# Router logits tied behind counted shared products, 2.5 units of shared work moved ahead of the last chunk's routing

## The chip, the cores and the metric

The kernel runs on one core of a Trainium2 chip. The metric is device time in microseconds (us), the median of three timed executions. Besides these there is one execution under the hardware profiler, from which all views of the profile come. Engines are called PE (TensorE matrix products; PEld its weight loads), DVE (VectorE), ACT (ScalarE), POOL (GpSimd) and SP (SyncE).

## The reference

Input `x` is 16 x 256 rows of 256 numbers, 4096 rows in all. First a spiking layer changes `x`, then a mixture of experts with one shared expert is added to it. All is float32.

```python
rates = relu(x) * 0.001
c  = cond[:, None, :] + cumsum(rates, axis=1)      # along the 256 steps
fl = floor(c);  x = x + (fl - previous fl) / 0.001 # previous of step 0: floor(cond)

shared = silu(x @ w1) * (x @ w3) @ w2              # 256 -> 512 -> 256
s      = sigmoid(concat([x, cond]) @ router_W)     # 8 experts
top2   = top_k(s + router_bias, 2)
gates  = s[top2] / sum(s[top2])                    # 1/2 each if the sum is about 0
y_e    = gelu(x @ W1e[e]) @ W2e[e]                 # 256 -> 256 -> 256
out    = x + (shared + sum over top2 of gates * y_e) / 3
```

## The kernel before

The rows go in eight chunks of 512 (`NCHUNK`). Three kinds of work are interleaved on the engines.

`elementwise(i)` makes the spikes of a chunk: PE turns `x` (L294), ACT makes rates, DVE scans them, floors, differences and adds. The last step (L389, two halves) writes `x1`, with the features on the partitions.

`route(i)` is the routing of a chunk, as a generator that is advanced step by step: logits `pl` on PE (L535, 16 records), on DVE their bound `lt` (L544), a transpose `pn` on PE (L547), Exp on ACT (L551), the choice of two experts on DVE (L553 to L590, ending with `hot`), counts `pr` on PE (L596 to L602), transposes `px` of the rows on PE with copies to `x1t` on ACT (L618, L619), the places `at_i` on DVE (L624 to L632), and at last eight indirect DMAs on POOL (L636), which scatter rows with their tags to the buffer `xs` in device memory, grouped by expert. The tag column is copied by POOL out of `key_first` (L571, L573). `key_first`, `at_i` and `lt` lie in the pool `rt` with two buffers each.

The shared expert is one generator, `all_shared`: hidden products of chunk i (L659: four pairs of products a chunk, each pair followed by Silu on ACT, L669, and a product on DVE, L670), then output products of chunk i-1 (L686, with an addition on DVE, L697). `unit(n)` advances it by n units: a unit is one pair of hidden products of 512 columns (four calls of matmul, eight records of the profile, since a float32 product is two), or one half of a chunk's output (eight calls, sixteen records). There are 48 units, or 288 calls. Units are the filling with which PE is kept at work while other engines prepare something.

What sets the order: in the loop `for i in range(2, NCHUNK)` the framework's scheduler orders each engine's instructions. It takes them by their place in the program and by when it thinks their inputs are ready, so a product that stands later in the program may be put ahead. The start and the last part stand under `manual_schedule`, where PE, DVE and ACT keep the written order. Each engine then runs its list strictly in order: an instruction that waits holds all behind it.

The last part begins with the routing of chunk 7: its logits, 0.5 unit, the score transpose and the choice, 2 units, counts, then `pcnt` (L866), the number of rows of each expert. From it DVE makes a table of blocks of 128 rows of one expert (L873 to L917), PE spreads it (`pcode` L920, `prow` L924), and SP writes eight pieces of zeros behind the experts' rows (L883). Between the table and `pcode` stand 2.5 units, behind `prow` 3 units, and one more in `run_blocks`. Then come 67 blocks: loads `xb` of a block from `xs` in four DMAs on SP and ACT (L956), which have to wait for the scatters' landing and the table; on DVE a copy of weights (L971) and a transpose `xbt` (L976); products `phe` (L1003); Gelu on ACT (L1011); products `py` (L1025); an indirect DMA of the result on POOL (L1034). A tail does the remaining units and adds everything up.

Of the kernel before, what the change touches and what calls it, by code (L numbers as in the profile page):

```python
# [13 lines left out]
F32 = mybir.dt.float32  # L14
BF16 = mybir.dt.bfloat16
I32 = mybir.dt.int32
# [15 lines left out]
P = 128  # L32
N = 512
SEG = 16
TOPK = 2
# [3 lines left out]
def kernel(  # L39
# [34 lines left out]
    J = N // P  # L74
    G = KD * NB
    NCHUNK = NT // N
    NTT = NT // P
    NSEG = T // SEG
    NBLK = NT * TOPK // P + E - 1
# [438 lines left out]


    placed = {}  # L520

    def route(i):
        x1, x1t = x1s[i], x1ts[i]

        def small(tag, shape=(P, J, E), dt=F32):
            return rt.tile(list(shape), dt, tag=tag, name=f"{tag}_{i}")

        def wide(a):
            return a[:, :, None].to_broadcast([P, J, E])


        pl = p_t.tile([P, P], F32, tag="pt", name=f"pl_{i}")
        for k in range(KD):
            for j in range(J):
                nc.tensor.matmul(  # L535
                    pl[ts(j, 32), :],
                    lhsT=rw[:, k, :],
                    rhs=x1[:, k, ts(j, P)],
                    start=(k == 0),
                    stop=(k == KD - 1),  # L540
                )
        yield
        lt = small("lt", (P, P))
        nc.vector.tensor_scalar(lt, pl, rc[:, i : i + 1], LOWEST, ALU.add, ALU.max)  # L544
        yield
        pn = p_t.tile([P, J, 32], F32, tag="pt", name=f"pn_{i}")
        nc.tensor.transpose(pn.rearrange("p j e -> p (j e)"), lt, ident)  # L547

        s = sig[:, ts(i, J), :]
        ex = small("ex")  # L550
        nc.scalar.activation(ex, pn[:, :, :E], AF.Exp, scale=-1.0)  # L551
        yield
        nc.vector.tensor_scalar(ex, ex, 1.0, None, ALU.add)  # L553
        nc.vector.reciprocal(s, ex)
        sel = small("sel")
        nc.vector.tensor_tensor(sel, s, rb[:, None, :].to_broadcast([P, J, E]), ALU.add)

        def best_places(sc, q):

            best = small(f"best{q}", (P, J))  # L560
            nc.vector.tensor_reduce(best, sc, AX.X, ALU.max)
            key = small(f"key{q}")
            nc.vector.tensor_tensor(key, sc, wide(best), ALU.is_equal)
            return key


        hots = [chosen[:, q, ts(i, J), :] for q in range(TOPK)]
        key = best_places(sel, 0)
        nc.vector.tensor_tensor(key, key, order, ALU.mult)
        key_first = small("first", (P, J))  # L570
        nc.vector.tensor_reduce(key_first, key, AX.X, ALU.max)  # L571
        nc.vector.tensor_tensor(hots[0], key, wide(key_first), ALU.is_equal)
        nc.gpsimd.tensor_copy(  # L573
            x1t[:, :, :, FQ + 1], key_first[:, :, None].to_broadcast([P, J, NQ])
        )
        sel2 = small("sel2")
        nc.vector.scalar_tensor_tensor(sel2, hots[0], -BIG, sel, ALU.mult, ALU.add)
        key = best_places(sel2, 1)
        run = small("run")
        nc.vector.tensor_tensor_scan(  # L580
            run.rearrange("p j e -> p (j e)"),
            keep_e,
            key.rearrange("p j e -> p (j e)"),
            0.0,
            ALU.mult,
            ALU.add,
        )
        nc.vector.scalar_tensor_tensor(hots[1], run, 1.0, key, ALU.is_equal, ALU.mult)
        hot = small("hot", dt=BF16)
        nc.vector.tensor_tensor(hot, hots[0], hots[1], ALU.add)  # L590
        yield

        pr = p_t.tile([P, J, E], F32, tag="pt", name=f"pr_{i}")
        nc.tensor.matmul(pr, lhsT=ones_r, rhs=region[0:1], start=True, stop=False)  # L596
        nc.tensor.matmul(pr, lhsT=before_b, rhs=hot, start=False, stop=False)
        for d in range(1, J):
            nc.tensor.matmul(
                pr[:, d:, :], lhsT=ones_b, rhs=hot[:, : J - d, :], start=False, stop=False  # L600
            )
        nc.tensor.matmul(  # L602
            pr,
            lhsT=ones_b,
            rhs=counts_b[i % 2][:, None, :].to_broadcast([P, J, E]),
            start=False,
            stop=True,
        )
# [13 lines left out]
        yield  # L622
        mine = small("mine", (P, TOPK, J, E))
        nc.vector.tensor_tensor(  # L624
            mine,
            chosen[:, :, ts(i, J), :],
            pr[:, None].to_broadcast([P, TOPK, J, E]),
            ALU.mult,
        )
        at_i = small("at_i", (P, TOPK, J), I32)  # L630
        with nc.allow_low_precision(reason="one whole number and zeros are added"):
            placed[i] = nc.vector.tensor_reduce(at_i, mine, AX.X, ALU.add)  # L632
        yield
        for j in range(J):
            for q in range(TOPK):
                nc.gpsimd.indirect_dma_start(  # L636
                    out=xs_w[(i * J + j) * TOPK + q][:, :],
                    out_offset=bass.IndirectOffsetOnAxis(ap=at_i[:, q, j : j + 1], axis=0),
                    in_=x1t[:, j].rearrange("p g f -> p (g f)"),
                    in_offset=None,  # L640
                )
        yield
# [5 lines left out]
    def shared_hidden(i, slices):  # L648

        ht = hts[i] = hid.tile([P, KS, N], F32, tag="ht", name=f"hs_{i}")  # L650
        x1 = x1s[i]
        for cols in slices:
            n = cols.stop - cols.start
            for u in range(KS):
                ps = []
                for w in (w1_sb, w3_sb):
                    ph = p_h.tile([P, n], F32, tag="ph", name=f"ph_{i}_{u}_{cols.start}_{len(ps)}")
                    for k in range(KD):
                        nc.tensor.matmul(  # L659
                            ph,  # L660
                            lhsT=w[:, k, ts(u, P)],
                            rhs=x1[:, k, cols],
                            start=(k == 0),
                            stop=(k == KD - 1),
                        )
# [11 lines left out]
    def shared_out(i):  # L677
# [4 lines left out]
        for h in range(J // n):  # L682
            pa = p_acc.tile([P, n, D], F32, tag="acc", name=f"pa_{i}_{h}")
            for q in range(n):
                for s in range(KS):
                    nc.tensor.matmul(  # L686
                        pa[:, q, :],
                        lhsT=ht[:, s, ts(n * h + q, P)],
                        rhs=w2_sb[:, s, :],
                        start=(s == 0),  # L690
                        stop=(s == KS - 1),
                    )
                yield 0.5, q == n - 1
# [135 lines left out]
    for i in range(2, NCHUNK):  # L829
# [12 lines left out]
        next(el, None)  # L842
        next(ro)
        next(nxt, None)
        unit(1 + (i > 3 and i % 3 != 2) + (i == NCHUNK - 1))
        next(ro)
        next(el, None)
        next(ro)
# [60 lines left out]
    table = const.tile([P, 2], I32)  # L909
    nc.vector.tensor_copy(table, table_f)  # L910

    diag = const.tile([P, P], BF16)
    nc.vector.tensor_scalar(which, which, -1.0, float(E), ALU.mult, ALU.add)
    nc.vector.tensor_scalar(diag, ident, which, None, ALU.mult)

    rows_f = const.tile([P, NBLK], F32)
    nc.vector.tensor_scalar(rows_f, ident[:, :NBLK], table_f[:, 0:1], None, ALU.mult)  # L917
    unit(2.5)
    pcode = p_t.tile([P, NBLK], F32, tag="pt", name="pcode")
    nc.tensor.matmul(pcode, lhsT=ones_b, rhs=diag[:, :NBLK], start=True, stop=True)  # L920
    code = const.tile([P, NBLK], F32)
# [2 lines left out]
    nc.tensor.matmul(prow, lhsT=ones_f, rhs=rows_f, start=True, stop=True)  # L924
    rows_i = const.tile([Q, NBLK + 1], I32)
    nc.vector.tensor_copy(rows_i[:, :NBLK], prow)
    unit(3)


    block, groups, first_rows = {}, {}, {}  # L930
# [269 lines left out]
```

## Time and profile before

| what | value |
|---|---|
| median of three timed runs | 332.89 us (332.87 to 333.72) |
| the profiled execution's own time | 342.67 us |
| its span, first to last instruction | 341.0 us |
| PE busy | 326.5 us, 96% |
| DVE busy | 225.3 us, 66% |
| ACT, POOL busy | 142.1 us, 162.8 us |
| chain that ended last: PE, DVE, ACT | 68%, 16%, 5% |
| first logits of chunks 2 to 7 on PE, at | 51.0, 69.5, 88.1, 102.8, 117.9, 136.5 us |
| first block product at | 170.3 us |
| hidden and output products of the tail, from | 292.8 us |

Times in the profile are counted from the first instruction. The profiled execution is some 10 us longer than the timed ones, so a wait that it shows need not be in these. A busy engine is one with an instruction running; for PE the matmuls' ends are modelled. In brackets behind an instruction stands how long its engine was idle before it, and what released it. "issue" means a wait for nothing that the profile shows.

### The profile page before, as it was taken

Reading aid. Unit: us, or ns where it says so; the run is one execution under the profiler, and the core shown is the slowest. Engines: PE = TensorE matmul, PEld = TensorE weight load, DVE = VectorE, ACT = ScalarE, POOL = GpSimd, SP = SyncE. Lnnn points to the kernel's source line nnn. Section 1 sums busy time; section 2 is a strip of 40 time slices with the busy share of each in tenths; the row PEclk is TensorE's granted clock in tenths of the full one; section 3 lists DMA queues with packets and bytes.
Section 4 is the critical chain, followed back from the end, with each engine's and each line's share of the span. In section 5 each row is a group of like instructions: output and inputs, shape, how many; then the busy total and the mean of one; then the engine's idle time right before and its main releaser. Section 6 shows DMA issues by size and latency. Waiting matters only on the chain.

```text
span 341.0 us, 6640 instructions
## 1 busy us (share of the span) xinstructions
PE 326.5 (96%) x1734; PEld 238.1 (70%) x1734; DVE 225.3 (66%) x612; ACT 142.1 (42%) x301; POOL 162.8 (48%) x199
## 2 busy tenths in 40 slices
PE   8899999789999999999999999999999989999996
PEld 3878544435654754855789999999999879566485
DVE  5787889677999896552277755554554543079993
ACT  4449394709487563041044444444443434310200
POOL 6000762766668887344035555555555445323220
PEclk9999999959999999999999999999999999999999
DMA  7570847643221222134446666675666553399933
GB/s 228 161 180 8 233 111 171 189 141 106 100 80 63 95 81 79 64 111 157 75 89 149 156 143 156 152 165 120 158 141 156 127 138 86 92 377 405 407 132 123
DMA packets 62550, 50.36 MB, mean 148 GB/s; under 512 B 42622, under 2 KB 52879, under 8 KB 62512
## 3 DMA queue, kind: packets, MB, share of 16 engines
q1 hardware_dynamic: 42928, 26.21, 30.0%
q0 software_dynamic: 7456, 20.86, 16.8%
q10 hardware_dynamic: 12128, 2.86, 4.8%
q8 instruction: 15, 0.25, 0.3%
q14 instruction: 23, 0.19, 0.2%
HBM read 27.44 MB, written 22.84 MB: 147 GB/s over the span
## 4 chain that ended last, share of the span: by engine, by line
PE 68%; DVE 16%; ACT 5%; issue 4%; DMA 2%; SPq 2%; another core or an unknown queue 1%; ACTq 0%; DVEq 0%
PE ph L659 21%; PE py L1025 15%; PE phe L1003 14%; PE pa L686 13%; DMA xb<-xs 2%; DVE tb L323 2%; SPq L956 2%; ACT tb L347 2%; DVE x L381 2%; DVE x L389 1%; DVE hs L670 1%; DVE tb L337 1%; PE pl L535 1%; ACT L551 1%; PE px L618 1%
## 5 line engine op out<-in xcount | busy, mean ns | idle before, releaser
L659 PE MATMUL ph<-x,w_sb 128*128 128x512 f32 (+2 forms) x320 | 121.2, 520 | 1.7 <-DVE x L487 0.8
L1034 POOL DMA_INDIRECT ys<-yb,to x67 | 66.4, 991 | 69.4 <-ACT yb L1033 51.9
L636 POOL DMA_INDIRECT xs<-x1t,at_i x64 | 76.5, 1195 | 46.4 <-issue 18.3
L659 PEld LDWEIGHTS ph<-x,w_sb 128*128 128x128 f32 x320 | 54.3, 193 | 45.0 <-issue 39.2
L1003 PEld LDWEIGHTS phe<-xbt,w1e 128*128 128x128 f32 x536 | 70.3, 191 | 4.7 <-ACT hbt L1011 0.9
L1003 PE MATMUL phe<-xbt,w1e 128*128 128x128 f32 x536 | 70.7, 275 | 0.7 <-DVE xbt L976 0.7
L1025 PE MATMUL py<-we,hbt 128*128 x268 | 69.1, 381 | 2.3 <-ACT hbt L1011 2.3
L686 PE MATMUL pa<-w_sb,hs 128*128 128x256 f32 x256 | 59.7, 383 | 0.0
L971 DVE COPY w1e<-we 128x512 f32 x67 | 29.1, 434 | 44.4 <-issue 29.9
L686 PEld LDWEIGHTS pa<-w_sb,hs 128*128 128x128 f32 x256 | 47.4, 190 | 9.5 <-issue 3.8
L669 ACT ACTIVATE as<-ph 128x512 f32<-128x512 f32 (+2 forms) x40 | 20.5, 515 | 73.8 <-PE ph L659 66.9
L1025 PEld LDWEIGHTS py<-we,hbt 128*128 128x128 f32 x268 | 45.8, 191 | 6.3 <-ACT hbt L1011 2.7
L1011 ACT ACTIVATE hbt<-phe 128x256 f32<-128x256 f32 x67 | 25.8, 385 | 47.5 <-ACT yb L1033 21.2
L670 DVE TENSOR_TENSOR hs<-as,ph 128x512 f32<-128x512 f32 (+2 forms) x40 | 23.0, 574 | 29.8 <-PE ph L659 20.7
L1033 ACT COPY yb<-py 128x256 f32<-128x256 f32 x67 | 25.0, 372 | 23.3 <-issue 17.4
L976 DVE STREAM_TRANSPOSE xbt<-xb 128x256 f32<-128x256 f32 x67 | 29.3, 437 | 1.3 <-DMA xb<-xs 0.7
L323 DVE TENSOR_TENSOR_SCAN tb<-keep,rates 128x1024 f32<-128x1024 f32 (+1 forms) x9 | 17.3, 1925 | 0.0
L712 POOL DMA_DIRECT2D out_dram<-yc x8 | 5.8, 727 | 22.7 <-DVE yc L1141 22.7
L573 POOL COPY x1t<-first 128x16 f32<-128x16 f32 x8 | 4.2, 526 | 25.0 <-DVE first L571 25.0
L347 ACT ACTIVATE tb<-tb,cond_t 128x256 f32<-128x256 f32 x30 | 13.1, 498 | 6.4 <-DVE tb L337 6.4
L697 DVE SCALAR_TENSOR_TENSOR x1t<-pa,x1t 128x512 f32<-128x512 f32 x14 | 9.6, 684 | 8.2 <-PE pa L686 8.2
L619 ACT COPY x1t<-px 128x512 f32<-128x512 f32 x16 | 8.9, 586 | 7.3 <-PE px L618 7.3
(152 smaller groups left out, 279.5 us busy)
## 6 DMA issues: line engine op xcount, KB each, us to landing
xb<-xs SPq DMA_DIRECT2D x184, 33.0 KB
yc<-ys SPq DMA_DIRECT2D x8, 512.0 KB
we<-ys SPq DMA_DIRECT2D x8, 512.0 KB
xn<-in_x_dram SPq DMA_DIRECT2D x7, 512.0 KB
xb<-xs ACTq DMA_DIRECT2D x84, 33.0 KB
we<-in_L_cond_W1e_dram SPq DMA_DIRECT2D x8, 256.0 KB
we<-in_L_cond_W2e_dram SPq DMA_DIRECT2D x8, 256.0 KB
out_dram<-yc POOLq DMA_DIRECT2D x8, 256.0 KB
```

The source lines that it names most:

```text
L323: nc.vector.tensor_tensor_scan(cs, keep[:, : cs.shape[1]], self.cut(self.rates, part), 0.0, ALU.mult, ALU.add)
L636: nc.gpsimd.indirect_dma_start(out=xs_w[(i * J + j) * TOPK + q][:, :], out_offset=bass.IndirectOffsetOnAxis(ap=at_i[:, q, j : j + 1], axis=0),
L659: nc.tensor.matmul(ph, lhsT=w[:, k, ts(u, P)], rhs=x1[:, k, cols], start=(k == 0), stop=(k == KD - 1),)
L670: nc.vector.tensor_tensor(ht[:, u, cols], act, ps[1], ALU.mult)
L686: nc.tensor.matmul(pa[:, q, :], lhsT=ht[:, s, ts(n * h + q, P)], rhs=w2_sb[:, s, :], start=(s == 0), stop=(s == KS - 1),)
L971: nc.vector.tensor_copy(w, we[:, bass.ds(off, KD * HE)])
L976: nc.vector.transpose(xt.rearrange("p g k r -> p g (k r)"), block[b].pop("xb")[:, :, :FQ])
L1003: nc.tensor.matmul(ph[:, m, :].rearrange("p (g r) -> p g r", r=Q), lhsT=w[:, k, ts(m, P)], rhs=xt[:, :, k, :], start=(k == 0), stop=(k == ...
L1011: nc.scalar.activation(ht, ph, AF.Gelu)
L1025: nc.tensor.matmul(py, lhsT=ht[:, k, :], rhs=we[:, bass.ds(off + KD * HE + k * D, D)], start=(k == 0), stop=(k == KH - 1),)
L1033: nc.scalar.copy(yb, py)
L1034: nc.gpsimd.indirect_dma_start(out=ys_w[b][:, :], out_offset=bass.IndirectOffsetOnAxis(ap=to[:, b : b + 1], axis=0), in_=yb, in_offset=Non ...
```

## The change

Four things are done.

1. Every shared product is counted as it is written down (`made`). The logits of chunks 2 to 6 get an order-only dependency on a counted product: chunk 2 comes behind the 84th, chunk 3 behind the 100th, then the 120th, 140th and 156th. No semaphore and no instruction is added; it binds the scheduler's order on PE.
2. In the loop, iterations with `i > 2` take half a unit more: 2.5 units over five iterations. The last part takes 2.5 less: 1.5 in place of 2.5 ahead of `pcode`, 1.5 in place of 3 behind `prow`. All of the loop's units stand ahead of the last chunk's logits on PE.
3. `key_first` and `at_i` get eight buffers in place of two.
4. `diag` and `rows_f` take buffers of the tag `lt` in place of their own.

```diff
+    logits = {i: [] for i in range(NCHUNK)}
+    STEP = {2: 84, 3: 100, 4: 120, 5: 140, 6: 156}
+    made = []
+
+    def in_step(i):
+        if i in STEP and logits[i] and len(made) >= STEP[i]:
+            for m in logits[i]:
+                tc.add_manual_dep(
+                    m.ins,
+                    made[STEP[i] - 1].ins.name,
+                    mybir.DependencyInfo(
+                        mybir.DependencyClass.NoSync, mybir.DependencyReason.DATA
+                    ),
+                    reason="order on TensorE",
+                )
+
+    def shared_matmul(*args, **kwargs):
+        made.append(nc.tensor.matmul(*args, **kwargs))
+        for i, n in STEP.items():
+            if n == len(made):
+                in_step(i)
...
-                nc.tensor.matmul(
+                logits[i].append(nc.tensor.matmul(
...
+        in_step(i)
         yield
...
-        key_first = small("first", (P, J))
+        key_first = small("first", (P, J), bufs=NCHUNK)
...
-        at_i = small("at_i", (P, TOPK, J), I32)
+        at_i = small("at_i", (P, TOPK, J), I32, bufs=NCHUNK)
...
-                        nc.tensor.matmul(
+                        shared_matmul(
                             ph,
...
-                    nc.tensor.matmul(
+                    shared_matmul(
                         pa[:, q, :],
...
-        unit(1 + (i > 3 and i % 3 != 2) + (i == NCHUNK - 1))
+        unit(1 + (i > 2) / 2 + (i > 3 and i % 3 != 2) + (i == NCHUNK - 1))
...
-    diag = const.tile([P, P], BF16)
+    diag = rt.tile([P, P], BF16, tag="lt", name="diag")
...
-    rows_f = const.tile([P, NBLK], F32)
+    rows_f = rt.tile([P, NBLK], F32, tag="lt", name="rows_f")
...
-    unit(2.5)
+    unit(1.5)
     pcode = p_t.tile([P, NBLK], F32, tag="pt", name="pcode")
...
-    unit(3)
+    unit(1.5)
```

More of the change, by code (lines that the diff above doesn't have):

```diff
@@ L520, with small @@
     placed = {}
+    logits = {i: [] for i in range(NCHUNK)}
[17 more added lines that the diff above has]
+                in_step(i)
     def route(i):
         x1, x1t = x1s[i], x1ts[i]
-        def small(tag, shape=(P, J, E), dt=F32):
-            return rt.tile(list(shape), dt, tag=tag, name=f"{tag}_{i}")
+        def small(tag, shape=(P, J, E), dt=F32, **kw):
+            return rt.tile(list(shape), dt, tag=tag, name=f"{tag}_{i}", **kw)
         def wide(a):
@@ L534, in route @@
             for j in range(J):
[L535 to L540, printed above, removed]
+                logits[i].append(
+                    nc.tensor.matmul(
+                        pl[ts(j, 32), :],
+                        lhsT=rw[:, k, :],
+                        rhs=x1[:, k, ts(j, P)],
+                        start=(k == 0),
+                        stop=(k == KD - 1),
+                    )
                 )
+        in_step(i)
         yield
```

## The prediction

> **What bounds the kernel now.** I read the page's head first, then TensorE's busy time stretch by stretch, then the timeline of each engine round the edited places, and last the row of one line. All fences are of the profiled execution of the kernel before.
>
> The head of the page, and two stretches of the table by windows (columns: stretch, its length, then busy time of PE, PEld, DVE, ACT, POOL with counts, granted clock, DMA share, GB/s):
>
> ```profile
> span 341.0 us, 6640 instructions
> PE 326.5 (96%) x1734; PEld 238.1 (70%) x1734; DVE 225.3 (66%) x612; ACT 142.1 (42%) x301; POOL 162.8 (48%) x199
> ...
> 60.00:70.00 10.00, 6.91 (x33) 3.63 (x30) 6.52 (x20) 5.74 (x10) 5.92 (x7) 0.95 0.76 206
> 70.00:80.00 10.00, 10.00 (x37) 4.68 (x36) 6.36 (x11) 3.49 (x7) 8.13 (x6) 0.70 0.31 110
> ```
>
> TensorE is the bound: 14.5 us idle in 341. The clock column gives what else it lost: 0.95 and 0.70 over two stretches of 10 us mean 1 + 6 = 7 us at half speed, so 3.5 us. The change adds and removes no product, so it can only move these 18 us.
>
> **The profiled execution is not the timed one.** It took 342.67 us, of which 1.7 lie outside the span; the median is 332.89, so a timed span is near 331.2, which is 9.8 us less. Matmuls at full clock can't get shorter, so those 9.8 us are idle and slow-clock time that timed runs don't have. Of the 18 us, the start (2.2 us in the first 10 us, 0.2 after) and the tail (3.2 us) make 5.6 that the program's shape forces. That leaves 18.0 - 9.8 - 5.6 = **2.6 us of TensorE idle** in a timed run between 20 and 338 us: nothing in the middle can gain more. One stall shows what was lost in the profile alone; the timeline of PE round the edits follows (start, length, line, what, count, [idle before <- releaser]):
>
> ```profile
> 65.62 1.02 PE L659 MATMUL ph<-x,w_sb 128*128 128x512 f32 x2
> 69.50 0.64 PE L535 MATMUL pl<-x,rw 128*32 128x128 f32 x4 [2.86 <-DVE at_i L632]
> ...
> 117.88 0.41 PE L535 MATMUL pl<-x,rw 128*32 128x128 f32 x4 [0.81 <-DVE x L389]
> ...
> 136.46 0.65 PE L535 MATMUL pl<-x,rw 128*32 128x128 f32 x16
> ...
> 145.97 0.40 PE L596 MATMUL pr<-region,ones_r 1*128 1x32 f32 x2
> ...
> 147.38 8.83 PE L659 MATMUL ph<-x,w_sb 128*128 128x512 f32 x20
> 156.04 0.20 PE L920 MATMUL pcode<-diag,ones_b 128*128 128x71 bf16 x1
> ...
> 156.41 3.70 PE L659 MATMUL ph<-x,w_sb 128*128 128x512 f32 x8
> 159.95 7.07 PE L686 MATMUL pa<-w_sb,hs 128*128 128x256 f32 x32
> 166.85 3.60 PE L659 MATMUL ph<-x,w_sb 128*128 128x512 f32 x8
> 170.29 1.05 PE L1003 MATMUL phe<-xbt,w1e 128*128 128x128 f32 x8
> 172.08 1.13 PE L1003 MATMUL phe<-xbt,w1e 128*128 128x128 f32 x8 [0.74 <-DVE xbt L976]
> ```
>
> The logits of chunk 3 stood 2.86 us in the middle of a hidden product, and the slow clock followed: 2.86 + 3.5 = 6.4 us. It cannot be in the timed runs: 5.6 + 6.4 alone would need 12 of the 18 - 9.8 = 8.2 us there are.
>
> The other engines at the hand-over from routing to the expert blocks, from their timelines, and the SP row of the loads' line (shortest/median/longest ns, first and last start):
>
> ```profile
> 131.58 1.29 DVE L389 SCALAR_TENSOR_TENSOR x<-x,xt 128x512 f32<-128x512 f32 x2
> ...
> 148.47 0.97 POOL L636 DMA_INDIRECT xs<-x1t,at_i  x1 [6.54 <-DVE ends L890]
> ...
> 157.40 0.97 POOL L636 DMA_INDIRECT xs<-x1t,at_i  x1 [0.30 <-issue]
> ...
> L956 SPq DMA_DIRECT2D xb<-xs x184: 3/316/1857, 160.0 to 282.3; - x184
> ```
>
> Spikes of the last chunk are ready at 132.87, but its logits run at 136.46, behind a backlog of shared products. From there a chain runs: logits, choice, places (147.0), eight scatters on POOL (148.47 to 158.37), their landing, block loads from 160.0, transpose, first block product. Shared products cover it on TensorE.
>
> **The parts, and their cost.**
>
> *Unit price.* 20 hidden records take 8.66 us (147.38 to 156.04), 0.433 each; 32 of L686 take 6.9, 0.216 each. A unit is 8 of the first or 16 of the second: 3.46 us. 2.5 units are **8.65 us**. Each hidden unit also carries one Silu on ACT (0.52) and one product on DVE (0.57 to 0.69), each output unit a DVE addition (0.68); no DMA goes with them here. ACT and DVE, 42% and 66% busy, hide these; uncovered, the 2.5 units' DVE part would be about 1.7 us.
>
> *Ties.* An order on one engine issues nothing. Counting calls (two records each) down the PE rows, logits of chunks 2 to 6 ran after 76, 90, 107, 122 and 140 shared products; they must now come after 84, 100, 120, 140 and 156, which is 5.2, 6.9, 9.1, 10.4 and 12.1 us more of shared work ahead (0.865 a hidden call, 0.432 an output call). Behind them on TensorE come the score transpose, the counts and the px transposes; for these wait Exp on ACT, the choice on DVE, and eight scatters on POOL (8 x 1.27 = 10.2 us a chunk). Late next: chunk 6's places move from 128.4 to about 140, so its scatters end near 150; the last chunk's start near 157. That cover is 7 us. Gain: the 0.81 before chunk 6's logits surely goes. The waits for `hot` before the counts (0.55, 0.23, 0.39) and one of 0.17 before a score transpose need not. Bounds: 0 to 2.15 us gained; a new static order could equally lose 1. I take **-0.8**.
>
> *A tile per chunk.* The rows of L571 and L632 show 0.7 and 0.2 us of idle in all over eight chunks each, and no DMA as releaser: nothing to gain, **0**. diag and rows_f take over `lt` buffers, last read by the score transpose at 138.86; diag is written at 150.48, rows_f at 150.68, with 11 us to spare: 0.
>
> *2.5 units moved.* The logits of the last chunk are written out behind all loop units: they move from after 160 calls to after 178, the cover of the chain shrinks by the same work (1 unit before pcode, 1.5 behind it), and the total is unchanged. Cover before: 136.46 to 170.29 = 33.8 us. After: 33.8 - 8.65 = **25.2**. Need: SP issues block 0's three loads from 160.02 to 161.92, and a load lands about 1.6 us after its issue (first update of the 160.02 load at 161.59); 0.5 for the transpose gives 164.0, so 164.0 - 136.46 = **27.6 us**. This need does not shrink: choice (hot ends 143.2) is still hidden by the two units ahead of pr, though Exp comes some 1.2 us later behind a Silu, and POOL's ten us are serial. So TensorE waits 27.6 - 25.2 = **+2.4 us** at the first block. Slack before was 6.3; that is what hid it. The wait of 0.74 at block 1 stays: DVE does block 0's transpose, then a shared product, then block 1's copy in the written order. Moved past: the scatters on POOL, eight zero stores and 184 loads on SP, 84 loads on ACT all start 8.65 us later against TensorE's work.
>
> *What is late next.* After the hand-over no slack is left. SP's 184 issues span 122.3 us, 0.668 each; 11 serve four blocks, so 1.84 us a block, against 1.76 for TensorE (174.07 to 175.83 between block products). Over 66 blocks SP loses 5.3 us of the old 6.3, harmlessly. SP's own waits for landings are 4.4 us of it; without them it keeps 1.77. So this costs 0 (SP keeps up when not profiled) to 5.3. I take **+1.2**, near the low end, since longest issues of 1.9 us against a median of 0.3 look like single delays and not its pace.
>
> *Clock.* [...] a gap of 2.86 us was followed by 7 us at half speed. [...] by the row it would cost another 3.5. I take 0[...] and keep 3.5 for the range.
>
> **Sum:** -0.8 + 2.4 + 1.2 = **+2.8**: on the profile's own terms 341.0 to 343.8 if its other stalls came again, and on the timed median 332.9 + 2.8 = **335.7 us**.
>
> **Rivals.**
> 1. *Clock or loads make it worse* (slower): the wait at block 0 reaches 2.9 us, the clock halves as at 69 us: +2.8 + 3.5 = +6.3, 339.2; with all of SP's 5.3 in place of 1.2, 343. For it: the row at 69 us. [...]
> 2. *The cover still suffices* (no change): chain and cover differ by 2.4 in 27.6. If untraced POOL and SP issues run 10% quicker, wait and drain vanish and -0.8 stays: about 332.1 to 333.5. Against: the 0.97 us of a scatter is DMA-issuing work that repeats to 10 ns.
> 3. *Faster*: timed runs do stand at the logits of chunks 3 to 6, and the 9.8 us come from elsewhere, such as the start. Place: TensorE before L535; price up to 6.4. It decides once more than 3.6 us of it is in timed runs (2.4 + 1.2); all of it gives 332.9 + 3.6 - 6.4 = 330.1. Against: the count of 2.6 us above.
>
> **Numbers.** A timed change under 0.3% (1.0 us; the runs spread over 0.85) can't be told from none. Forecast 0.50 (own range 334 to 338), rival 1 0.21, rival 2 0.17, rival 3 0.12. Faster 0.12, same 0.17, slower 0.71. The range leaves out most of rival 3 and the end of rival 1: 331.5 to 340.5.
>
> **What would show it.** Right: last logits near 144 to 145; first load on SP near 168; idle of 2 to 3 us before the first phe, released by the transpose or by xb loads; later block products waiting on hbt or xbt behind loads; no L535 idle over 0.3. Wrong: no idle at the first phe (need overstated), or idle before the last logits released by x L389 (then the extra units fill a hole I count as none), or new idle inside the loop behind scores or counts.

## The result, and the profile after

The changed kernel takes **344.87 us** (median of four runs, 344.52 to 346.02), the kernel before 332.99 beside it: a ratio of **1.0357**, 95% interval 1.0338 to 1.0375, so 11.9 us slower. 335.7 was forecast, with a range to 340.5. The direction was right, and the place in part: the hand-over to the expert blocks, but neither the wait that grew most nor the chunk loop. The size was off by a factor of four. Three of the later runs (marked "disturbed" below) fell on executions in which the kernel before itself took 335 to 343 us and a stall of some 3 us stood in the chunk loop.

Head of the page after, and two stretches of the table by windows (stretch, length, busy PE, PEld, DVE, ACT, POOL, granted clock, DMA share, GB/s):

```profile
span 342.8 us, 6638 instructions
...
PE 325.5 (95%) x1734; PEld 238.9 (70%) x1734; DVE 225.1 (66%) x612; ACT 143.0 (42%) x301; POOL 156.8 (46%) x199
...
160.00:170.00 10.00, 7.67 (x30) 4.79 (x29) 1.85 (x4) 0.00 (x0) 2.37 (x3) 0.97 0.44 108
170.00:180.00 10.00, 5.90 (x22) 5.25 (x23) 4.31 (x14) 3.17 (x6) 1.00 (x1) 0.52 0.42 70
```

The work is the same, 1734 products. What is new lies between 166 and 180 us: TensorE idles for over 6 us and then has a granted clock of 0.52. The changed kernel's lines stand 24 to 26 further down than before (logits L535 → L559, score transpose L547 → L573, block product L1003 → L1029), except that all shared products, L659 and L686, are now recorded at the helper's line L540. TensorE's timeline:

```profile
69.99 0.18 PE L623 MATMUL pr<-hot,before_b 128*128 128x32 bf16 x1 [0.79 <-DVE hot L616]
...
87.49 0.18 PE L623 MATMUL pr<-hot,before_b 128*128 128x32 bf16 x1 [1.07 <-DVE hot L616]
...
139.68 0.64 PE L559 MATMUL pl<-x,rw 128*32 128x128 f32 x16
143.44 0.30 PE L573 MATMUL pn<-ident,lt 128*128 128x128 f32 x1 [1.20 <-DVE lt L570]
...
162.85 3.60 PE L540 MATMUL ph<-x,w_sb 128*128 128x512 f32 x8
168.36 1.23 PE L1029 MATMUL phe<-xbt,w1e 128*128 128x128 f32 x8 [1.92 <-DVE xbt L1002]
174.00 2.05 PE L1029 MATMUL phe<-xbt,w1e 128*128 128x128 f32 x8 [4.41 <-DVE xbt L1002]
```

Four groups of waits: for `hot` in the chunk loop, 1.20 us at the last chunk's score transpose, 1.92 at the first block product (2.4 were forecast), and **4.41 at the second**, where 0.74 had stood. The product behind it runs at half speed: 2.05 us for what took 1.13 in the kernel before.

The second wait is read from the other engines' timelines round the hand-over (POOL's first and last scatter of chunk 7, then ACT, then DVE):

```profile
153.05 0.98 POOL L662 DMA_INDIRECT xs<-x1t,at_i  x1 [6.31 <-DVE ends L916]
...
162.00 0.97 POOL L662 DMA_INDIRECT xs<-x1t,at_i  x1 [0.30 <-issue]
...
164.46 7.29 ACTq L982 DMA_DIRECT2D xb<-xs  x7
171.85 0.60 ACT L695 ACTIVATE as<-ph 128x512 f32<-128x512 f32 x1 [17.30 <-DMA xb<-xs]
...
167.86 0.45 DVE L1002 STREAM_TRANSPOSE xbt<-xb 128x256 f32<-128x256 f32 x1 [3.23 <-DMA xb<-xs]
172.48 0.69 DVE L696 TENSOR_TENSOR hs<-as,ph 128x512 f32<-128x512 f32 x1 [4.17 <-ACT as L695]
173.08 0.42 DVE L997 COPY w1e<-we 128x512 f32 x1
173.42 0.44 DVE L1002 STREAM_TRANSPOSE xbt<-xb 128x256 f32<-128x256 f32 x1
```

From the bottom up: block 1's transpose at 173.42 stands behind the copy and the shared expert's product `hs` in VectorE's list; `hs` waits for the Silu `as`; the Silu could have run near 164.8 (it needs the first half of the `ph` products, some 1.9 us from their start, as the next fence shows), but it stands in ScalarE's list behind **seven block loads**, the early ones of `run_blocks`. These wait for the scatters: the first starts at 164.46, 1.49 us behind the end of the last one on POOL (162.97), and the seven take 7.29 us to issue. So seven DMA issues hold up one Silu by 7.1 us, and through VectorE's order a block product that does not use it. That is **theory Q** of the expectations. **Theory C** is its companion: the clock that the idle brings down costs a few us more (2.0 us, measured below).

The same place in the kernel before, from a second profile of it unchanged (span 331.7, clock 1.0; two lines each of ACT, DVE and PE):

```profile
153.10 5.71 ACTq L956 DMA_DIRECT2D xb<-xs  x7
161.86 0.60 ACT L669 ACTIVATE as<-ph 128x512 f32<-128x512 f32 x1 [9.74 <-DMA xb<-xs]
...
163.65 0.69 DVE L670 TENSOR_TENSOR hs<-as,ph 128x512 f32<-128x512 f32 x1 [1.62 <-PE ph L659]
...
164.58 0.44 DVE L976 STREAM_TRANSPOSE xbt<-xb 128x256 f32<-128x256 f32 x1
...
159.94 3.60 PE L659 MATMUL ph<-x,w_sb 128*128 128x512 f32 x8
...
165.17 1.13 PE L1003 MATMUL phe<-xbt,w1e 128*128 128x128 f32 x8 [0.74 <-DVE xbt L976]
```

There ScalarE was through with its seven early loads at 158.81, 3.05 us ahead of the Silu. **That slack of 3.05 us on ScalarE is what the change used up**; the 6.3 us of slack in the prediction were those of SP and the first transpose. The loads now start 11.36 us later (153.10 to 164.46) and the shared products ahead of the Silu only 2.91 (159.94 to 162.85), so against TensorE's list the loads have moved by 8.45 us, about the price of the units. The seven issues also take 1.58 us longer (7.29 against 5.71). That makes 8.45 + 1.58 - 3.05 = 7.0 us late, where the trace has 7.1.

**The ledger**, by the idle in the trace after against that second profile of before. TensorE's idle from 20 to 300 us went from 3.16 to 12.37 us: +2.5 in the chunk loop (5.24 - 1.55 up to 150 us, less the 1.20 that comes next), +1.20 at the last score transpose, +1.92 at the first block product, +3.67 at the second (4.41 - 0.74). That is 9.3; the half clock adds some 2 (measured below). 11.3 in all, where the spans differ by 11.1 and the medians by 11.9.

### The profile page after: what moved, and what is told of

It is laid out like the page before. It is cut to its first block, busy times and chain, and to the rows that moved or that the text cites. A ratio compares the mean times of both kernels' runs of the same rounds, so it can differ in the third digit from the quotient of the medians.

```text
span 342.8 us, 6638 instructions
## 1 busy us (share of the span) xinstructions
PE 325.5 (95%) x1734; PEld 238.9 (70%) x1734; DVE 225.1 (66%) x612; ACT 143.0 (42%) x301; POOL 156.8 (46%) x199
## 3 DMA queue, kind: packets, MB, share of 16 engines
q10 hardware_dynamic: 12128, 2.86, 4.8%
## 5 line engine op out<-in xcount | busy, mean ns | idle before, releaser
L540 PE MATMUL ph<-x,w_sb 128*128 128x512 f32 (+2 forms) x320 | 118.5, 513 | 1.1 <-ACTq L1124 0.7
L662 POOL DMA_INDIRECT xs<-x1t,at_i x64 | 69.7, 1089 | 58.2 <-issue 15.9
L540 PEld LDWEIGHTS ph<-x,w_sb 128*128 128x128 f32 x320 | 53.9, 190 | 45.2 <-issue 38.8
L1029 PEld LDWEIGHTS phe<-xbt,w1e 128*128 128x128 f32 x536 | 71.9, 196 | 10.9 <-issue 4.6
L1029 PE MATMUL phe<-xbt,w1e 128*128 128x128 f32 x536 | 72.5, 279 | 6.3 <-DVE xbt L1002 6.3
L1051 PE MATMUL py<-we,hbt 128*128 x268 | 69.8, 384 | 0.1
L540 PE MATMUL pa<-w_sb,hs 128*128 128x256 f32 x256 | 59.3, 381 | 0.0
L540 PEld LDWEIGHTS pa<-w_sb,hs 128*128 128x128 f32 x256 | 47.5, 190 | 8.9 <-issue 3.2
L599 POOL COPY x1t<-first 128x16 f32<-128x16 f32 x8 | 5.4, 674 | 23.4 <-DVE first L597 23.3
```

Source lines behind the costliest of these rows:

```text
L540: made.append(nc.tensor.matmul(*args, **kwargs))
L662: nc.gpsimd.indirect_dma_start(out=xs_w[(i * J + j) * TOPK + q][:, :], out_offset=bass.IndirectOffsetOnAxis(ap=at_i[:, q, j : j + 1], axis=0),
L1029: nc.tensor.matmul(ph[:, m, :].rearrange("p (g r) -> p g r", r=Q), lhsT=w[:, k, ts(m, P)], rhs=xt[:, :, k, :], start=(k == 0), stop=(k == ...
L1051: nc.tensor.matmul(py, lhsT=ht[:, k, :], rhs=we[:, bass.ds(off + KD * HE + k * D, D)], start=(k == 0), stop=(k == KH - 1),)
```

## The experiments

Where an expectation speaks of theory Q or C, these are the two above. The runs go from the parts of the change to the hand-over, not in order of time. Ratios are against the kernel before, run beside each.

### The kernel before again

No edit; it asks what the profiled execution had that timed runs don't.

> The kernel before, unchanged, for a profile that is closer to its timed runs. All theories: 332.9 us. If the profiled execution is near 333 too, the wait of 2.86 us at the logits of chunk 3 and the 7 us of half clock behind it should be missing, and the idle of PE between 20 and 300 us should add up to 2 to 4 us. If the wait is there again in an execution of 333 us, my count of what timed runs can hold was wrong.

Measured: 333.1 against 333.07, ratio 1.0003 (0.9994 to 1.0012), span 331.7. The stall of 2.86 us ahead of chunk 3's logits and the slow clock behind it are gone, and idle between 20 and 300 us is 3.16, where the prediction had worked out 2.6. Products at full clock take as long in both profiles (8.83 us for the twenty hidden records ahead of `pcode`). So that stall belonged to one execution, and rival 3 had nothing to win.

### Tiles alone

```diff
-    STEP = {2: 84, 3: 100, 4: 120, 5: 140, 6: 156}
+    STEP = {}
-        unit(1 + (i > 2) / 2 + (i > 3 and i % 3 != 2) + (i == NCHUNK - 1))
+        unit(1 + (i > 3 and i % 3 != 2) + (i == NCHUNK - 1))
-    unit(1.5)
+    unit(2.5)
-    unit(1.5)
+    unit(3)
```

(Against the changed kernel, as all diffs here.)

> Eight buffers for key_first and at_i and the moved diag and rows_f alone; no ties, units as before. All theories: nothing, 332.6 to 333.3. If the order made for this kernel differs by chance it can be off by a us.

Measured: 332.6, ratio 0.9984 (0.9977 to 0.9991). The tiles give 0.5 us at most.

### Ties and tiles, units where they were

The same edit without the line of `STEP`.

> The changed kernel with its 2.5 units put back behind the last chunk's routing; ties and tiles stay. Theory A (the hand-over costs it: 2.5 units less cover for the last chunk's chain): the first two block products wait as before, no half clock at 170 us, 333 to 336, where the part over 333 is what the ties cost in the loop (waits of the counts on hot). Theory R (the ties cost it, by a worse order in the loop): 340 or more.

Measured: 334.8, ratio 1.0045 (1.0026 to 1.0063): the ties **cost 2.2 us** (334.8 - 332.6). The granted clock averages 1.00 over the run, and the second block product waits its old 0.74. TensorE's timeline has the loss in the chunk loop, whose idle up to 150 us is 3.50 where the tiles alone have 1.24:

```profile
69.98 0.18 PE L623 MATMUL pr<-hot,before_b 128*128 128x32 bf16 x1 [0.78 <-DVE hot L616]
...
87.38 0.18 PE L623 MATMUL pr<-hot,before_b 128*128 128x32 bf16 x1 [0.97 <-DVE hot L616]
...
110.75 0.30 PE L573 MATMUL pn<-ident,lt 128*128 128x128 f32 x1 [0.86 <-DVE lt L570]
```

The logits don't wait, but in the kernel before, profiled again, they didn't either: the 0.81 us that the prediction let the ties win was not there. What follows the logits waits more. For chunk 2's counts (69.98) the cover is thinner: 16 records of shared products stand between its last logits and them, against 22 in the kernel before, by TensorE's timelines. For chunk 3's (87.38) it is not: 30 records against 18. There the choice itself takes longer on VectorE: 7.7 us from its first step (`ex`, 79.61) to the end of `hot` (87.33), where the kernel before took 6.1 (72.70 to 78.76). Two instructions of `elementwise` for a later chunk stand between its steps:

```profile
82.48 2.29 DVE L323 TENSOR_TENSOR_SCAN tb<-keep,rates 128x1024 f32<-128x1024 f32 x1 [0.26 <-ACT rates L301]
...
85.13 1.16 DVE L337 TENSOR_TENSOR tb<-tb,tot 128x960 f32<-128x960 f32 x1
```

In the kernel before, two others stand there, of 1.20 and 1.23 us. So later logits meet other work on VectorE; that this costs the time is read off the timeline, and no run moved these instructions.

### The same ties, at the places where the logits stood

```diff
-    STEP = {2: 84, 3: 100, 4: 120, 5: 140, 6: 156}
+    STEP = {2: 76, 3: 91, 4: 108, 5: 122, 6: 141}
```

with the units put back as above. It asks whether an order written out by hand costs by itself.

> Tiles, units as before, and ties at the places where the logits stood without them, rounded up to whole hidden products: 76, 91, 108, 122, 141 in place of 84, 100, 120, 140, 156. If the ties cost through the shift of the logits (8 to 18 products later), PE's idle before the counts in the loop returns to 1.2 to 1.6 us and the time to 332.4 to 333.2. If a tie costs as such, by a worse order, 334 or more as with the ties of the change.

Disturbed: 339.09 against 337.46, ratio 1.0086 (1.0045 to 1.0127), with a wait of 3.03 us at a shared product that no other run has. Nothing follows from it for the time. Again:

> Tiles per chunk and the ties, at the places where the logits stood before (behind 76, 91, 108, 122 and 141 shared products), and no unit moved. If the loss from the ties lies in how late they put the logits: about 332.6 to 333, that is the time of the tiles alone. If an order written out by hand costs by itself: near 334.8, as with the ties at 84 to 156.

Measured: 332.19 against 333.04, ratio 0.9974 (0.9963 to 0.9984), no worse than the tiles alone. Chunk 2's counts (64.48) wait 0.17, and chunk 3's, at 81.04, not at all:

```profile
64.48 0.18 PE L623 MATMUL pr<-hot,before_b 128*128 128x32 bf16 x1 [0.17 <-DVE hot L616]
...
81.04 0.18 PE L623 MATMUL pr<-hot,before_b 128*128 128x32 bf16 x1
```

So a tie is free; **putting the logits 8 to 18 shared products later** is what costs 2.2 us.

### Units and tiles, no ties

```diff
-    STEP = {2: 84, 3: 100, 4: 120, 5: 140, 6: 156}
+    STEP = {}
```

> The changed kernel without ties: the 2.5 units are moved and the tiles are there, the scheduler orders the logits as it likes. Theory A: PE idles about 2 us before the first block product and 4 to 5 before the second, half clock for some 10 us, 341 to 345. Theory R: 336 or less.

Measured: 342.25, ratio 1.0266 (1.0234 to 1.0298): the units **cost 9.65 us** (342.25 - 332.6). Parts add up: 332.6 + 2.2 + 9.65 = 344.4, against 344.87. The hand-over is that of the changed kernel, 2.5 us earlier; ScalarE's timeline:

```profile
161.92 6.99 ACTq L982 DMA_DIRECT2D xb<-xs  x7
169.01 0.60 ACT L695 ACTIVATE as<-ph 128x512 f32<-128x512 f32 x1 [16.97 <-DMA xb<-xs]
```

The first block product waits 2.11, the second 3.96, and the granted clock averages 0.985 over the run's 340.6 us, by estimate some 10 us at half speed. All of the large loss is in the units.

### One and a half units in place of two and a half

```diff
-        unit(1 + (i > 2) / 2 + (i > 3 and i % 3 != 2) + (i == NCHUNK - 1))
+        unit(1 + (i > 4) / 2 + (i > 3 and i % 3 != 2) + (i == NCHUNK - 1))
-    unit(1.5)
+    unit(2)
-    unit(1.5)
+    unit(2)
```

with `STEP = {}`. Moving 1.5 units takes 5.2 us of cover, less than the 6.3 of slack that the prediction had found.

> Tiles, no ties, and 1.5 units moved in place of 2.5 (half a unit in each of the last three iterations; 0.5 less ahead of pcode, 1 less behind). Shift of the chain against the cover: 5.2 us. Theory Q: PE's slack at the first block is 6.3, so no wait there; ACT's last early load would end about 5.2 later than 158.8 while the unit's products end at 161.4, so the Silu comes some 2.5 us late, and block 1's product about 1 to 2.5 us: 333.5 to 335, and no half clock. A theory of a cost in proportion to the units (9.6 us for 2.5): 338.4.

Measured: 339.55, ratio 1.0204 (1.0184 to 1.0224), a miss of the expected time by over 4 us. What was right: the first block product does not wait. But the second waits 2.71, the first down product 0.94 (for Gelu, behind the same loads on ScalarE), the last score transpose 1.13, and the granted clock averages 0.990 over the run's 337.7 us, by estimate some 6.8 us at half speed. So 5.2 us of moved cover, which costs nothing by SP's slack, cost 7 (1.13 of it at the score transpose, the rest behind ScalarE's loads and by the clock), since ScalarE had only 3.05. It is the shorter slack that counts.

### A unit written one turn later: in the kernel before, and in the changed one

If the Silu and `hs` are in the way of block 1's transpose, writing the unit behind that transpose must win the 0.74 us which even the kernel before loses. With ties and units put back as above (tiles alone):

```diff
-            if b == 0:
+            if b == 1:
                 unit(1)
```

> Tiles alone (no ties, units as before), and the unit inside the block loop is written behind the second block's transpose in place of ahead of its weight copy. PE's order stays; on DVE the unit's product then stands behind block 1's copy and transpose. If the 0.74 us wait before the second block product comes from DVE's order, it goes: 331.9 against 332.6 for the tiles alone, which would be 0.3% under the kernel before. If not: 332.6.

Measured: **331.79, ratio 0.9965 (0.9952 to 0.9977)**, as expected, and faster than both kernels. VectorE, then TensorE:

```profile
161.93 0.44 DVE L1002 STREAM_TRANSPOSE xbt<-xb 128x256 f32<-128x256 f32 x1
163.28 0.69 DVE L696 TENSOR_TENSOR hs<-as,ph 128x512 f32<-128x512 f32 x1 [0.91 <-PE ph L540]
...
163.01 1.95 PE L1029 MATMUL phe<-xbt,w1e 128*128 128x128 f32 x16
```

The second transpose goes ahead of `hs`, and both blocks' products run in one piece.

The same one line in the changed kernel:

> The changed kernel, with the unit in the block loop written one turn later, so that its Silu and its VectorE product stand behind the second block's transpose. Theory Q (the wait of 4.41 us at the second block product is the Silu behind seven loads on ScalarE, handed on by VectorE's order): the second transpose no longer waits for the Silu, so the second block product waits 0 to 0.8 us. ScalarE still issues its seven loads, then the Silu, then the first Gelu, so the first down product waits for that Gelu instead, 1.5 to 2.5 us. The wait of about 2 us at the first block product stays. In all 1.5 to 3 us less than the changed kernel: 342 to 343.5. Rival (the second product waits for its block's rows or for SP's loads): its wait stays at 4 to 4.5 us, released by xbt, and the time stays at 344.5 to 345.5.

Measured: 344.4, ratio 1.0335 (1.0317 to 1.0352), no better than the changed kernel; the expectation missed, and the rival too. TensorE, ACT, DVE:

```profile
175.22 2.08 PE L1029 MATMUL phe<-xbt,w1e 128*128 128x128 f32 x8 [5.61 <-ACT as L695]
...
164.50 9.96 ACTq L982 DMA_DIRECT2D xb<-xs  x9
174.57 0.60 ACT L695 ACTIVATE as<-ph 128x512 f32<-128x512 f32 x1 [19.96 <-DMA xb<-xs]
...
169.65 0.45 DVE L1002 STREAM_TRANSPOSE xbt<-xb 128x256 f32<-128x256 f32 x1 [0.76 <-DMA xb<-xs]
```

The second transpose is done at 170.1, 5 us before the product that uses it. But a turn later there are **nine** loads ahead of the Silu, it comes 2.7 us later, and the block product now waits for the Silu itself (`as`, which has to read `ph` before its accumulator is free for another product; that this is the reason is inferred from the releaser and from the pool `p_h`, whose three buffers the shared pair and block 0 fill). The loads and rows are in time; the Silu behind loads is what binds. In the kernel before the same edit wins because ScalarE had slack.

### Fewer loads ahead of the Silu

```diff
-    AHEAD = 6
+    AHEAD = 3
```

> The changed kernel, but only three blocks' loads stand ahead of the block loop in place of six, so four loads and not seven stand before the Silu on ACT. SP's order of loads stays. Theory Q (the 4.4 us wait before the second block product is ACT's list: Silu behind seven loads, DVE's product behind Silu, block 1's copy and transpose behind that): the Silu starts near 167 in place of 171.9, the wait at block 1 falls to about 1, PE keeps its full clock, 338 to 340. Theory L (block 1's data land late): wait and clock stay, 344 to 346.

Measured: 351.25, ratio 1.0521 (1.0487 to 1.0555), far above what was expected. At the hand-over it does what theory Q says: four loads, the Silu 4.6 us earlier, and no wait at the second block product (ACT):

```profile
164.50 2.60 ACTq L982 DMA_DIRECT2D xb<-xs  x4
167.21 0.60 ACT L695 ACTIVATE as<-ph 128x512 f32<-128x512 f32 x1 [12.62 <-DMA xb<-xs]
```

But a lead of three blocks holds for the whole stage, and is too short: the groups of lines have 11.6 us of wait at block products, 9.2 of it at eight of them later than 190 us, behind transposes that wait for rows (columns: busy us, mean ns, idle before).

```profile
L1029 PE MATMUL phe<-xbt,w1e 128*128 128x128 f32 x536 | 73.2, 281 | 11.6 <-DVE xbt L1002 11.5
...
L1002 DVE STREAM_TRANSPOSE xbt<-xb 128x256 f32<-128x256 f32 x67 | 29.6, 442 | 33.5 <-DMA xb<-xs 32.7 <-SPq L1124 0.3
```

The edit did two things at once, so the next one keeps the lead of the rest of the stage.

### Loads spread over the first turns

```diff
-        for b in range(first, min(first + AHEAD, end)):
+        ready = min(first + 3, end)
+        for b in range(first, ready):
             load_block(b, first, end)
...
-            if b + AHEAD < end:
-                load_block(b + AHEAD, first, end)
+            for _ in range(2):
+                if ready < end and ready <= b + AHEAD:
+                    load_block(ready, first, end)
+                    ready += 1
```

> The changed kernel with three blocks' loads ahead of the block loop and then two blocks' loads per turn of the loop, until six blocks are ahead again. It keeps what e5_ahead3 showed at the hand-over (Silu at 167, no wait at the second block product) and not its short lead. Theory Q with the clock as seen: the wait at the first block product stays at about 2, that at the second is under 0.5, half clock for one or two steps of 3.4 us, and no row of waits afterwards: 338.5 to 341. If the loss of e5_ahead3 had another cause than the short lead, waits in the block stage come again: over 345.

Disturbed: 353.95 against 337.46, ratio 1.0526 (1.038 to 1.067); the second block product waits 0.70, and many down products wait later. Inconclusive, and made again beside the changed kernel itself:

> The changed kernel again, on the chip of the two runs that follow, so that they can be set against it: 344 to 346, with a wait of 1.9 us at the first block product, 4.4 at the second, and the half clock for 10.24 us.

The changed kernel: 344.79, ratio 1.0352 (1.0326 to 1.0377). The waits are as expected (1.92 and 4.03), and the granted clock averages 0.990 over 342.4 us, by estimate some 6.8 us at half speed and not 10.24.

> The changed kernel with three blocks' loads ahead of the block loop and two more at every turn until the lead of seven is reached, again on a quieter chip. Theory Q: the second block product waits under 0.8 us, the half clock is one step of 3.41 us; 339 to 341 if the loads keep up. Rival (the 6 us of waits at the hand-over also gave the loads their lead): waits on loads return through the block stage, and the time is 344 or more.

Measured: **340.55, ratio 1.0225 (1.0195 to 1.0256), 4.2 us less than the changed kernel**, as theory Q had it. ACT, DVE, PE:

```profile
164.50 2.60 ACTq L982 DMA_DIRECT2D xb<-xs  x4
167.20 0.60 ACT L695 ACTIVATE as<-ph 128x512 f32<-128x512 f32 x1 [12.62 <-DMA xb<-xs]
...
170.25 0.45 DVE L1002 STREAM_TRANSPOSE xbt<-xb 128x256 f32<-128x256 f32 x1 [0.74 <-DMA xb<-xs]
...
168.66 1.16 PE L1029 MATMUL phe<-xbt,w1e 128*128 128x128 f32 x8 [2.19 <-DVE xbt L1002]
170.84 2.05 PE L1029 MATMUL phe<-xbt,w1e 128*128 128x128 f32 x8 [1.02 <-DVE xbt L1002]
```

With four loads ahead of the Silu the second wait is 1.02 (the transpose now waits for the block's rows, no longer for `hs`), the half clock is down to 3.4 us (by estimate from a mean of 0.83 over 170 to 180 us), and after that TensorE loses only 0.17 us to the block stage up to 290 us: the loads keep up. Only the places of the loads in the lists were changed.

### The Silu ahead of all loads

```diff
-    unit(1.5)
+    unit(2.5)
...
-            if b == 0:
-                unit(1)
```

The first line is the unit count nearest ahead of the block loads.

> The changed kernel with the unit of the block loop written ahead of all block loads (behind the last of the units ahead of the loop), so that its Silu stands ahead of ScalarE's seven early loads; loads, ties and the sum of the units are as in the changed kernel. Theory Q: hs is ready before the first transpose, so the second block product waits 0.7 us or less (4.41 in the changed kernel, 5.61 where the Silu stood behind nine loads). The first block product still waits about 2 us. The first Gelu and its table load still stand behind the seven loads, to about 173.5, so the first down product waits some 2 to 3 us in place of none. In all 2 to 3 us less than the changed kernel: 342 to 343. Rival (the time is lost anyway, since the loads give back later what they don't win here): 344.5 to 346, with new waits on loads within the block stage.

Disturbed: 353.11 against 335.92, ratio 1.0474 (1.0376 to 1.0572), with a stall of 3.2 us at 85 us. Again, beside the two runs above:

> The unit of the block loop written ahead of all block loads, again (the first time its loads landed slowly and a stall stood at 85 us, ahead of anything that the edit touches). Theory Q: the second block product no longer waits for the Silu; 0.7 us or less if its rows land as in the changed kernel, up to 1.8 if they land as in the first run; the first down product waits 1 to 3 us for its Gelu behind the seven loads. In all 2 to 3 us less than the changed kernel on the same chip. Rival (the loads need that time anyway): as long as the changed kernel or longer, with new waits on loads within the block stage.

Measured: 344.12, ratio 1.0329 (1.0304 to 1.0353): 0.7 us less than the changed kernel where 2 to 3 were expected. ACT, DVE, PE:

```profile
164.79 0.60 ACT L695 ACTIVATE as<-ph 128x512 f32<-128x512 f32 x1 [10.21 <-PE ph L540]
166.37 6.56 ACTq L982 DMA_DIRECT2D xb<-xs  x9
...
171.03 0.45 DVE L1002 STREAM_TRANSPOSE xbt<-xb 128x256 f32<-128x256 f32 x1 [1.85 <-DMA xb<-xs]
...
171.63 2.05 PE L1029 MATMUL phe<-xbt,w1e 128*128 128x128 f32 x8 [1.71 <-DVE xbt L1002]
174.69 2.08 PE L1051 MATMUL py<-we,hbt 128*128 x4 [1.02 <-ACT hbt L1037]
```

The second wait falls from 4.03 to 1.71, and is of another kind. A list in order holds up either way: now ScalarE's loads stand behind the Silu, and start at 166.37 instead of 164.42. By that the rows of blocks 0 and 1 come later (first wait 2.28, second 1.71, both released by the transposes; the second of these waited 1.85 for its rows). The first Gelu, behind nine loads, holds up the down product by 1.02. Silu first is not the cure; loads in portions, as in the run above, are.

### What the half clock costs

Idle products (bf16, on `busy`, into a tile of their own; they belong to no result) fill the two waits, eight ahead of the first block product and eighteen ahead of the second:

```diff
+        if b < 2:
+            fill = p_t.tile([P, N], F32, tag="pt", name=f"fill_{b}")
+            for _ in range((8, 18)[b]):
+                nc.tensor.matmul(fill, lhsT=busy[:, :P], rhs=busy, start=True, stop=True)
```

> The changed kernel with 8 and 18 idle bf16 products of 0.216 us put before the first and the second block product, 1.7 and 3.9 us, so that PE is at work while it waits. They belong to no result. Theory C (the half clock at 169 us follows from the idle PE and costs half of the block products' time in it, 2.9 us): clock stays full, about 342. If the half clock has another cause, or costs nothing since the loads are late anyway: 344.5 to 346, or more.

Measured: 342.85, ratio 1.0306 (1.0285 to 1.0327). The eight idle products take 1.89 us and the eighteen 4.05, 0.216 us for each one more. The two stretches of the table by windows have a granted clock of 1.00:

```profile
160.00:170.00 10.00, 9.78 (x42) 5.90 (x41) 1.86 (x4) 0.00 (x0) 2.34 (x3) 1.00 0.43 109
170.00:180.00 10.00, 8.61 (x51) 6.13 (x49) 5.10 (x16) 3.82 (x8) 1.46 (x2) 1.00 0.47 80
```

So the half clock costs **2.0 us** (344.87 - 342.85). By estimate the trace after would allow 2.9 (10.24 us at half speed, less 4.5 idle within them, halved); the rest is hidden because the first down product then waits 1.39 us for its Gelu, which stands behind ScalarE's loads and starts at 175.54 us here, at 175.71 in the trace after.

## Why the prediction was wrong

By its own steps:

- **"The wait of 0.74 at block 1 stays: DVE does block 0's transpose, then a shared product, then block 1's copy in the written order."** This step failed. The order was read rightly, and the step moved "84 loads on ACT" on paper, but it never asked when the shared product's own input would be ready, that is, what stands ahead of the Silu in ScalarE's list. "ACT and DVE, 42% and 66% busy, hide these" took the share of busy time for slack. The slack stood in the profile that the prediction read: ScalarE's seven loads run from 160.01 to 165.21 there and the Silu at 168.77, so 3.56 us were left against 8.65 us moved. The wait became 4.41 us: +3.67. Shown by two runs: loads in portions bring it to 1.02 and the time down by 4.2 us, and two more loads ahead of the Silu lengthen it to 5.61.
- **Clock: 0.** The second half of the same error, +2.0. The forecast wait of 2.4 was taken to be too short to cost any clock, which was the author's estimate. It was 1.92, and the clock fell 0.96 us after it had ended (169.32), before the long stall. The 3.5 us kept for the range were enough for this alone.
- **Ties: -0.8.** The sign was wrong: +2.2. The loss lies where the prediction said that it "could equally lose 1", in counts and score transposes that now wait, and is no price of the ties as such (332.19 with the ties in place). The gain was read from a wait that only the one profiled execution had.
- **Choice "still hidden by the two units ahead of pr, though Exp comes some 1.2 us later behind a Silu".** The number came out by luck: the place and the cause were others, and it was not hidden. TensorE's own list has the score transpose ahead of those units, and that transpose waits for `lt`, not for Exp. `lt` now stands on VectorE behind a shared product `hs`, whose second `ph` TensorE makes only after the logits:

```profile
142.35 0.69 DVE L696 TENSOR_TENSOR hs<-as,ph 128x512 f32<-128x512 f32 x1 [3.58 <-PE ph L540]
142.95 0.34 DVE L570 TENSOR_SCALAR lt<-pl,rc 128x128 f32<-128x128 f32 x1
```

In the kernel before, output products follow the last logits, and `lt` runs 0.14 us behind these (130.33, logits to 130.19). With the units moved, a hidden pair is cut in two by the logits. TensorE stood 1.20 us, and the chain came that much later (24.8 us from the last logits to the first load, 139.68 to 164.46, against 23.6 before). It is the failed step once more, an instruction behind another one's wait in one list.
- **First block product: +2.4.** Right: 1.92. The cover of 25.2 and the need of 27.6 were the right pair, for SP's loads.
- **SP drain: +1.2.** No wait is seen: behind the hand-over the changed kernel's block stage does not wait up to 290 us. The 6.3 us of stall may have given the loads their lead back; no run shows it, and with loads in portions and 3.2 us of stall 0.17 us are lost. The run with a lead of three blocks shows what lies below it (11.6 us of wait at block products).
- **Tiles: 0.** Measured -0.5 at most.
- **2.6 us of idle in a timed run, and the stall of 2.86 us in the profile alone.** Right (3.16 measured), and with it the verdict on rival 3. Rival 1 named the clock rightly but kept the wrong wait, and ended at 343.

Sum: +2.5 (loop) + 1.2 + 1.9 + 3.7 + 2.0 = 11.3, where +2.8 was forecast.

What stays open: how much of the loss is the last of the seven issues. Six of them start between 164.46 and 168.68 us, the seventh only at 171.37. By the semaphore events it waits until 171.35 for the landing of a load that SP had issued at 169.10. Four issues take 2.60 us without such a wait, and the seven of the kernel before took 5.71. No run took that wait away. Nor were the 0.6 us left between ledger and medians traced.

## What to carry to other kernels

In these runs an engine that issues DMAs was a list in order: the Silu behind ScalarE's seven loads ran 7.1 us after it could have, for the loads waited for the scatters until 164.46 us, took 7.29 to issue, and the last one also waited for an earlier landing (until 171.35), though ScalarE was busy for 42% of the span. When cover is taken from a chain, work out the slack of **each** list that crosses the hand-over (here SP 6.3 us, ScalarE 3.05) and take the shortest, and ask of each instruction that stays put when its own inputs come. In this kernel early loads did best in portions between the computations of the same engine: all ahead of them cost 4.2 us more, all behind them 3.6 (344.79 and 344.12 against 340.55).

## What was not expected of the hardware

**The clock halved behind a wait of 1.92 us.** In the trace after, the granted clock is 1.00 up to 169.32 us, 0.50 from there to 179.56, and 1.00 again behind. In the 10 us ahead of the fall TensorE was idle for 1.92 us in all, the wait at the first block product. The fall came 0.96 us after this wait had ended, and 0.27 us ahead of the wait of 4.41. In the first profile of the kernel before, the clock fell at 69.07 us, 2.43 us into the wait of 2.86, and stayed at 0.50 for 6.83 us.

Two other runs have no wait near 4 us and the half clock too. With a lead of three blocks one wait of 2.27 us stands at the first block products, and the granted clock is 0.86 from 165 to 170 us and 0.90 from 170 to 180, by estimate 3.4 us at half speed. With loads in portions (waits of 2.19 and 1.02) it is 0.83 from 170 to 180, again some 3.4 us. In the kernel before again, with a wait of 0.74 at the second block product, it is 1.00 from 20 to 300 us.

The prediction took its wait of 2.4 us to cost nothing more, by its author's estimate. A wait of 1.92 was followed by the half clock here, and with idle products in both waits the clock stayed at 1.00 from 160 to 180 us and the time was 2.0 us shorter. What decides when the clock falls is not shown by these runs.

**The half clock did not last equally long with waits alike.** One profiled execution of the changed kernel had it for 10.24 us, another for some 6.8 (by estimate from its mean clock of 0.990 over 342.4 us), with the same wait of 1.92 at the first block product and 4.41 and 4.03 at the second. Why is not shown.
